# A transformer block on one core: exponentials behind the outputs, maxima ahead of them, a fifth stack, and operands at multiples of 128 bytes

## The chip, the cores and the metric

The kernel runs on one core of a Trainium2 chip. The metric is the device time of one launch in microseconds (us); lower is better. Before the change the median of three runs is 813.3 us (809.93 to 813.58).

## The reference: what is computed

One pre-norm transformer block in float32 on an input of 4 x 512 rows of 512. There are 32 heads of 16, with ALiBi slopes and a causal mask, and a gated feed-forward part with 1,376 inner columns. Cut to what matters:

```python
def block(x):
    n = layernorm(x)
    q, k, v = split(n @ w_attn + b_attn)                # 32 heads of 16
    s = einsum('bqhd,bkhd->bhqk', q, k) / 16
    s = where(rel <= 0, s + slopes * rel, -inf)         # rel = key - query
    x = x + einsum('bhqk,bkhd->bqhd', softmax(s), v) @ w_proj + b_proj
    n = layernorm(x)
    return x + (silu(n @ w_gate.T) * (n @ w_up.T)) @ w_down.T
```

## The kernel before

**Precision.** Every large product is made of three matmuls: each operand is split into a high and a low part (tiles of type float32r), and high x high, high x low and low x high are added in one PSUM bank. All matmuls are recorded under one helper, L86 (after the change L87), transposes under L89, so groups are told apart by tiles: xnT (normalized x, transposed), wqk_t, wrow_t (weights of v or of the projection), wf (feed-forward weights), c (q or k with bias), st (stacks), P (exponentials), v (values), aT (scaled heads), hl (the feed-forward part's inner rows).

**Units and steps.** A unit u (16 of them) is one batch and a quarter of the heads; each unit gives two steps su (32 in all, four heads each). A stack st holds, for the four heads of a step, rows of q and k and the rows that make the slopes and a coarse mask, so that one matmul of 64 rows gives the scores of a block. Two such matmuls, on rows 0 to 63 and 64 to 127, run side by side and write two banks. There are four stacks, used in turn.

**Two passes over the scores.** pass_a (L563) makes the scores of a step in five blocks of two banks each; VectorE adds the triangular mask and keeps each query's maximum (L582, into the tile M). Blocks 1 and 3 have 512 columns a bank, blocks 2 and 4 have 384 + 128, block 5 has 256 + 256. to_row (L590) transposes M on TensorE, copies it on ScalarE (tile mt) and writes it by a DMA on GpSimd's queue (L596) as one row into the step's stack. pass_b (L598) makes the scores again, transposed and with the maxima taken off by that row: five fills, each of two banks, two exponentials on ScalarE (L619) and two selects on GpSimd (L622) that clear what lies above the diagonal. Then av (L628) multiplies P with the values: 32 matmuls of a quarter of the array's columns (the outputs, tile U). Behind the outputs av issues what waits in `behind` (transposes of the next batch's x), the row of maxima of step su + 2, and the copy of U (tile ue) to DRAM.

**Jobs.** The projections of q, k and v and the output projection are jobs of 12 matmuls of 512 columns. Two jobs run as a pair (pair_steps, L362): each matmul is cut into two of 64 rows that run side by side, and the two jobs change their halves of the array in the middle. There a copy of one column (tile sync, L382) on ScalarE makes the second half wait for the first. in_step (L764) spreads the 24 pairs of matmuls over a step. qk_job (L401) ends with c in a high and a low part and sends it to DRAM (qd), from where load_stack (L513, on SyncE's queue) brings it into a stack; own_rows (L501, on GpSimd's queue) writes the rows that don't come from q and k.

**Heads and projection.** head_sums, inverses, attn_heads and scaled_heads read back U and the sums, multiply on GpSimd (uc by rb, L687), and make aT on ScalarE (L690) and VectorE (L691). proj_job (L457) adds bias and x.

**The feed-forward part.** For each batch, 11 tiles of gate, up and down weights (wf). Silu, product and the split into hl are L893, L897, L899 and L900; weights are loaded and split on the way (raw, L242 and L243). The first three tiles of the first batch run as pairs within steps 29 to 31, the others one matmul after another.

**What sets the order.** A list of events is written by hand: at(t, ...) gives each piece of work a time in units, of which a step has ten, and the events are issued in the order of these times. TensorE's instructions and SyncE's DMAs stay in that order (keep_in_program_order); on ScalarE, VectorE and GpSimd a scheduler may move what is not pinned. Each engine works through its queue in order. There are eight PSUM banks for everything. SBUF tiles come from pools; those that the change touches are t4 (c, xnT, aT, hl; 11 buffers of 4 KB a partition), P (13 of 2 KB), the stacks (4 of 8 KB), and the small tiles st (statistics, 24 bytes) and sync (4 bytes).

Within a step that starts at t0 = 10 su, the order in units is, before the change: block 1 of step su + 2 at -2.1, fill 1 at -0.9, block 2 at -0.2, the outputs of the step before at 0.5, then fill 2 (1.1), block 3 (2.1), fill 3 (3.1), block 4 (4.1), fill 4 (5.0), block 5 (6.0), fill 5 (6.9).

## Time and profile before

| what | value |
|---|---|
| runs (three) | 809.93, 813.58, 813.3 us; median 813.3 |
| the profiled execution | 814.1 us, of which the span from first to last instruction is 812.4 |
| mean granted clock of TensorE | 0.974 |
| attention: first outputs to last | 67.6 to 434.9 us of the span |
| feed-forward alone on TensorE | about 435 to 812 us |

Engines are PE = TensorE (PEld its weight loads), DVE = VectorE, ACT = ScalarE, POOL = GpSimd, SP = SyncE. Durations come from the one profiled execution. A busy time is a union: matmuls overlap, so one that is shown with 0.4 us may start 0.23 us after the one before. What a matmul costs is therefore read from the distance between starts. In views of stretches each engine's busy time stands before its number of records; then come the granted clock of TensorE (1.00 or 0.50 in single windows), the DMA share and GB/s. An idle time is shown with what ended it.

### The profile page before, as it was taken

The numbers are of one execution on the slowest core, as the hardware profiler recorded it, in microseconds if no ns is written. First come the engines' busy times: TensorE is split into PE (matmuls) and PEld (weight loads), VectorE is DVE, ScalarE is ACT, GpSimd is POOL, SyncE is SP. The second block draws the span as 40 slices with busy tenths as digits, with TensorE's granted clock in tenths as the row PEclk, the third lists the DMA queues.
The fourth block names the chain that finished last, engine by engine and source line by source line (L and its number), as shares of the span: only waits on it lengthen the run. The fifth ranks groups of instructions, "written<-read, shape, count | busy, mean of one in ns | idle before, by whom it ended". The sixth has DMA issues, their size and how long they took to land.

```text
span 812.4 us, 14957 instructions
## 1 busy us (share of the span) xinstructions
PE 779.6 (96%) x5272; PEld 587.4 (72%) x5272; DVE 458.5 (56%) x1441; ACT 343.0 (42%) x669; POOL 256.3 (32%) x560
## 2 busy tenths in 40 slices
PE   6998998999999999998999899999999999999997
PEld 5764755777777767765766688788887888788885
DVE  7798776988888888789833533621144121531212
ACT  4435665687656766674595322311112111211110
POOL 5415454666665566675533110000000000000000
PEclk9986998999999999998999999999999999999999
DMA  6444356458662776576335424221001101010001
GB/s 220 138 136 151 124 166 218 158 183 269 203 220 73 234 252 211 172 247 200 132 102 175 129 81 135 74 78 27 13 27 48 57 13 27 27 52 27 27 0 53
DMA packets 54764, 99.10 MB, mean 122 GB/s; under 512 B 13928, under 2 KB 14184, under 8 KB 54336
## 3 DMA queue, kind: packets, MB, share of 16 engines
q1 hardware_dynamic: 50464, 94.73, 35.9%
q0 software_dynamic: 4224, 3.40, 1.7%
q8 instruction: 42, 0.69, 0.3%
q14 instruction: 34, 0.28, 0.1%
HBM read 65.05 MB, written 32.77 MB: 120 GB/s over the span
## 4 chain that ended last, share of the span: by engine, by line
PE 84%; DVE 6%; DMA 3%; issue 2%; ACT 2%; POOL 2%; DVEq 0%; POOLq 0%; ACTq 0%
PE bank L86 81%; DVE bank L582 3%; PE bank L89 2%; DMA st<-mt 2%; ACT P L619 1%; DVE st L128 1%; DVE xt L145 1%; DVE M L582 1%; DMA ud<-ue 1%; POOL uc L687 0%; POOL P L622 0%; POOL r L135 0%; POOL xr L475 0%; DMA xt<-in_x 0%; DVE mv L129 0%
## 5 line engine op out<-in xcount | busy, mean ns | idle before, releaser
L86 PE MATMUL bank<-xnT,wf 128*128 128x512 f32 (+2 forms) x1128 | 270.7, 401 | 4.2 <-ACT sync L382 2.0
L582 DVE CUSTOM_DVE_ANT_0 bank<-bank,mask_t 128x512 f32<-128x512 f32 (+3 forms) x512 | 236.4, 520 | 35.0 <-PE bank L86 32.7
L86 PEld LDWEIGHTS bank<-xnT,wf 128*128 128x128 f32 (+2 forms) x1128 | 197.8, 188 | 54.1 <-ACT sync L382 2.7
L619 ACT ACTIVATE P<-bank 128x512 f32<-128x512 f32 x320 | 172.5, 598 | 66.9 <-PE bank L86 60.5
L86 PE MATMUL bank<-st 64*128 64x512 f32 (+3 forms) x1024 | 147.5, 327 | 13.9 <-DMA st<-mt 7.0
L897 DVE TENSOR_TENSOR sg<-sg,bank 128x512 f32<-128x512 f32 (+1 forms) x44 | 30.3, 688 | 208.8 <-PE bank L86 201.0
L622 POOL TENSOR_SCALAR_AFFINE_SELECT P<-P 128x256 f32<-128x256 f32 (+1 forms) x320 | 115.2, 366 | 102.5 <-ACT P L619 92.6
L86 PEld LDWEIGHTS bank<-st 64*128 64x128 f32 x1024 | 110.7, 190 | 44.9 <-DVE M L582 12.4
L86 PE MATMUL bank<-wf,hl 128*128 128x512 f32 (+1 forms) x528 | 136.2, 395 | 0.0
L86 PE MATMUL bank<-xnT,wqk_t 64*128 64x512 f32 (+1 forms) x720 | 116.9, 404 | 0.5 <-ACT sync L382 0.3
L86 PEld LDWEIGHTS bank<-wf,hl 128*128 128x128 f32 (+1 forms) x528 | 98.9, 188 | 23.5 <-issue 0.4
L893 ACT ACTIVATE sg<-bank 128x512 f32<-128x512 f32 (+1 forms) x44 | 26.3, 597 | 160.3 <-PE bank L86 160.2
L86 PE MATMUL bank<-P,v 128*32 128x512 f32 (+3 forms) x1024 | 84.8, 477 | 2.1 <-DVE M L582 1.8
L86 PEld LDWEIGHTS bank<-xnT,wqk_t 64*128 64x128 f32 (+1 forms) x720 | 72.0, 185 | 14.4 <-ACT sync L382 3.6
L899 ACT CAST hl<-sg 128x512 fp32r<-128x512 f32 (+1 forms) x44 | 27.3, 620 | 118.1 <-DVE sg L897 118.1
L582 DVE DVE_READ_ACCUMULATOR2_ANT M<- 128x1 f32 x512 | 72.1, 141 | 0.0
L133 POOL TENSOR_SCALAR ve<-mv 128x4 f32<-128x4 f32 x7 | 1.6, 225 | 209.1 <-DVE mv L129 209.1
L86 PEld LDWEIGHTS bank<-P,v 128*32 128x32 f32 x1024 | 32.2, 117 | 44.0 <-issue 36.8
L86 PE MATMUL bank<-wrow_t,aT 64*128 64x512 f32 (+1 forms) x336 | 63.8, 402 | 0.1
L86 PE MATMUL bank<-wrow_t,xnT 64*128 64x512 f32 (+1 forms) x336 | 59.1, 408 | 0.1
L900 DVE TENSOR_TENSOR hl<-sg,hl 128x512 fp32r<-128x512 f32 (+1 forms) x44 | 31.2, 710 | 28.2 <-ACT hl L899 27.8
L86 PEld LDWEIGHTS bank<-wrow_t,xnT 64*128 64x128 f32 (+1 forms) x336 | 37.9, 189 | 6.9 <-ACT sync L382 0.9
(77 smaller groups left out, 538.6 us busy)
## 6 DMA issues: line engine op xcount, KB each, us to landing
st<-qd SPq DMA_DIRECT2D x90, 256.0 KB, 3.8
qd<-c SPq DMA_DIRECT2D x30, 512.0 KB, 4.8
ud<-ue SPq DMA_DIRECT2D x32, 256.0 KB, 3.3
raw<-in_wgu SPq DMA_DIRECT2D x20, 256.0 KB, 3.2
xt<-in_x SPq DMA_DIRECT2D x16, 256.0 KB, 4.1
uc<-ud SPq DMA_DIRECT2D x16, 256.0 KB, 5.5
rb<-rd SPq DMA_DIRECT2D x16, 256.0 KB, 5.3
xr<-in_x SPq DMA_DIRECT2D x16, 256.0 KB, 4.7
```

The costliest lines, as they stand in the source:

```text
L86: tc.keep_in_program_order(nc.tensor.matmul(*args, **kw))
L89: tc.keep_in_program_order(nc.tensor.transpose(*args))
L128: pin(dve.bn_stats(st, xs[t]))
L133: pin(pool.tensor_scalar(ve, box["mv"][:, :, 1], EPS, None, ALU.add))
L145: dve.tensor_scalar(xs[t], xs[t], mv[:, t, 0:1], box["r1"][:, t : t + 1], ALU.subtract, ALU.mult)
L582: dve.tensor_tensor_reduce(s, s, mask_t[:, S - w : S], -1.0, 3.0e38, ALU.add, ALU.min, m[:, n : n + 1])
L619: act.activation(pt, p, AF.Exp)
L622: pool.affine_select(d, d, pattern=[[0, len(parts)], [1, 128]], compare_op=ALU.is_ge, fill=0.0, base=0, channel_multiplier=-1)
L893: act.activation(sg[:m], p, AF.Silu)
L897: dve.tensor_tensor(sg[:m], sg[:m], p, ALU.mult)
L899: act.copy(hl[:m, 0, :], sg[:m])
L900: dve.tensor_tensor(hl[:m, 1, :], sg[:m], f(hl[:m, 0, :]), ALU.subtract)
```

## The change

It has four parts.

1. The order in a step. Blocks of pass_a for step su + 2 move to -4.7, -2.5, -0.3, 0.9 and 3.1 units (relative to t0), the fills to 1.5, 2.6, 3.9, 4.9 and 6.3. So three blocks of two banks stand ahead of the outputs, and all five fills of a step behind the outputs of the step before.
2. Five stacks instead of four (NST), loaded for step su + 5 instead of su + 4, rows at t0 + 6.5 instead of 7.1 and q and k at t0 + 8.0 instead of 8.8. To make room, P has 12 buffers and t4 has 10.
3. One pair of jobs a step, in other steps than before. The pair of unit 3 is spread over step 0; the q and k of the next batch's four units lie in steps 2 to 5 of a batch (before: 2, 3, 4 or 5, and 9), the first two projections in steps 14 and 17, and 22 and 25 (before 13 and 14, 21 and 22), with the heads for them scaled 12 units later. Steps without a pair are 1, 6, 9 and 26; before, they were 1, 4, 6 and 26. From 280 units on the copy sync is made on VectorE. Some constants of the feed-forward part change: its first time (324.0 to 325.5), one weight load (318 to 314), and the times of the first three tiles' down matmuls (321, 323.9, 326.8 to 321, 331.3, 333.0).
4. The tiles st and sync are taken as 16 columns of which 6 and 1 are used, and an unused tile of 32 bytes, fill, is added. In the built program before, the tiles that matmuls read, ident and v apart, start 32 or 96 bytes past a multiple of 128 in their partition; after the change they start on one.

The arithmetic and the number of matmuls stay the same.

```diff
@@
-    'ffn': 324.0,
+    'ffn': 325.5,
...
-    't4': 11,
+    't4': 10,
...
-    'P': 13,
+    'P': 12,
@@ stats, norm
-            st = com.tile([128, 6], F32, tag="bst", bufs=2, name="st")
+            st = com.tile([128, 16], F32, tag="bst", bufs=2, name="st")[:, 0:6]
@@
+    cp.tile([128, 8], F32, name="fill")
@@ pair_steps
-                sync = com.tile([128, 1], F32, tag="sync", bufs=2, name="sync")
-                act.copy(sync, box["p"][1][:, 0:1])
+                sync = com.tile([128, 16], F32, tag="sync", bufs=2, name="sync")[:, 0:1]
+                (act.copy if clock["now"] < 280.0 else dve.tensor_copy)(sync, box["p"][1][:, 0:1])
@@
-    ST = [ph1.tile([128, 2, 2 * S], FR, name=f"st{n}") for n in range(4)]
+    ST = [ph1.tile([128, 2, 2 * S], FR, name=f"st{n}") for n in range(NST)]
@@ pass_b
-        for t, parts in zip((-0.9, 1.1, 3.1, 5.0, 6.9), fills):
+        for t, parts in zip((1.5, 2.6, 3.9, 4.9, 6.3), fills):
@@
+    at(1.0, load_stack, 4)
...
-    pairs(-1.8, 0.15, qk_job(3, 0), qk_job(3, 1))
@@
-        pass_a(su, (...)[su] if su < 2 else tuple(t0 - t for t in (22.1, 20.2, 17.9, 15.9, 14.0)))
+        pass_a(su, (...)[su] if su < 2 else tuple(t0 - t for t in (24.7, 22.5, 20.3, 19.1, 16.9)))
...
-        if su + 4 < NS:
-            at(t0 + 7.1, own_rows, su + 4)
-            at(t0 + 8.8, load_stack, su + 4)
+        if su + NST < NS:
+            at(t0 + 6.5, own_rows, su + NST)
+            at(t0 + 8.0, load_stack, su + NST)
@@
+        if not b:
+            in_step(0, qk_job(3, 0), qk_job(3, 1))
         if b:
             in_step(t, v_job(b, 2), v_job(b, 3))
-            in_step(t + 1, qk_job(4 * b + 3, 0), qk_job(4 * b + 3, 1))
         if b + 1 < B:
             xT_next(b + 1, 10.0 * (t + 1))
-            for n, s in enumerate((2, 3, 4 if b else 5)):
-                in_step(t + s, qk_job(4 * b + 4 + n, 0), qk_job(4 * b + 4 + n, 1))
+            for n in range(4):
+                in_step(t + 2 + n, qk_job(4 * b + 4 + n, 0), qk_job(4 * b + 4 + n, 1))
@@
-    for b, first, gap, s in ((0, 102.0, 5.0, 13), (1, 182.0, 5.0, 21), (2, 240.0, 5.5, 27)):
+    for b, first, gap, steps in ((0, 114.0, 5.0, (14, 17)), (1, 194.0, 5.0, (22, 25)), (2, 240.0, 5.5, (27, 28))):
...
-            in_step(s + n, proj_job(b, 2 * n), proj_job(b, 2 * n + 1))
+            in_step(steps[n], proj_job(b, 2 * n), proj_job(b, 2 * n + 1))
@@
-    for n, t in enumerate((262.0, 302.0, 271.0, 290.0, 318.0, 308.0)):
+    for n, t in enumerate((262.0, 302.0, 271.0, 290.0, 314.0, 308.0)):
@@ ffn
-            down(it, max(times[it] + PRM["ffs"] * 5 / 3, 321.0 + 2.9 * it))
+            down(it, times[it] + PRM["ffs"] * 5 / 3 if b or it >= PRM["fp"] else (321.0, 331.3, 333.0)[it])
```

More of the change, by code (lines that the diff above doesn't have):

```diff
@@ L27 @@
 KM = 47
+NST = 5
 FAR = -30000.0
@@ L176, in norm @@
             c = slice(t, t + 1)
-            st = com.tile([128, 6], F32, tag="bst", bufs=2, name="st")
+            st = com.tile([128, 16], F32, tag="bst", bufs=2, name="st")[:, 0:6]
             ov.bn_stats(st, xs[t])
@@ L501, in own_rows @@
     def own_rows(su):
-        st = ST[su % 4]
+        st = ST[su % NST]
         r0 = 8 * (su % 8)
-        assert su < 4 or used.get(su - 4) == 5
+        assert su < NST or used.get(su - NST) == 5
         for a in range(2):
@@ L507, in own_rows @@
             pin(pool.dma_start(to[3:16:4], cst[r0 + 4 * a : r0 + 4 * a + 4].rearrange("r (n c) -> r n c", n=2)))
-            if su < 4:
+            if su < NST:
                 pin(pool.dma_start(to[19:64:4], cst[64:76].rearrange("r (n c) -> r n c", n=2)))
-        if su >= 4:
+        if su >= NST:
             pin(pool.dma_start(st[KM : KM + 65 : 64, 0], cst[72:74, 0 : 2 * S]))
@@ L515, in load_stack @@
         u, s = divmod(su, 2)
-        assert {("qd", u, 0), ("qd", u, 1)} <= made and (su < 4 or used.get(su - 4) == 5)
+        assert {("qd", u, 0), ("qd", u, 1)} <= made and (su < NST or used.get(su - NST) == 5)
         src = qds[u].rearrange("n (e s l) c -> s e n (l c)", e=32, s=2)
-        st = ST[su % 4]
-        dma = (lambda *args: pin(sp.dma_start(*args))) if su < 4 else sp.dma_start
+        st = ST[su % NST]
+        dma = (lambda *args: pin(sp.dma_start(*args))) if su < NST else sp.dma_start
         for n, from_ in enumerate((slice(0, 4, 2), slice(0, 4, 3), slice(1, 3))):
@@ L556, in turn_stack @@
             own_rows(1)
-            for n in (2, 3):
+            for n in range(2, NST):
                 own_rows(n)
@@ L756, in block_kernel @@
         t0 = 10.0 * su
-        pass_a(su, ((-33.5, -19.5), (-19.0, -4.0))[su] if su < 2 else tuple(t0 - t for t in (22.1, 20.2, 17.9, 15.9, 14.0)))
+        pass_a(su, ((-33.5, -19.5), (-19.0, -4.0))[su] if su < 2 else tuple(t0 - t for t in (24.7, 22.5, 20.3, 19.1, 16.9)))
         if su < 2:
```

## The prediction

> **What bounds the kernel now.** I read the page first, then the spans step by step, then the waits of TensorE, then single stretches of its timeline.

> ```profile
> PE 779.6 (96%) x5272; PEld 587.4 (72%) x5272; DVE 458.5 (56%) x1441; ACT 343.0 (42%) x669; POOL 256.3 (32%) x560
> ...
> PEclk9986998999999999998999999999999999999999
> ```

> TensorE is busy for 96% of the span, so at most 33 us are idle. But busy time also holds matmuls at half clock, and matmuls that come more slowly than they could; the second row shows where the clock is cut. The next view cuts the span at the first output matmul (P,v) of each step. Columns: TensorE, weight load, VectorE, ScalarE, GpSimd busy, then clock.

> ```profile
> 102.60:110.90 8.30, 7.08 (x71) 4.10 (x67) 8.05 (x33) 6.70 (x15) 5.87 (x16) 1.00 0.70 249
> ...
> 123.50:133.70 10.20, 7.56 (x71) 4.44 (x70) 8.78 (x36) 6.90 (x15) 7.16 (x17) 0.91 0.88 293
> 133.70:148.40 14.70, 13.89 (x119) 9.04 (x120) 9.46 (x38) 7.62 (x17) 5.82 (x14) 0.83 0.34 122
> ...
> 195.80:208.00 12.20, 11.84 (x114) 8.82 (x115) 10.11 (x37) 8.60 (x18) 8.37 (x16) 1.00 0.55 182
> 208.00:219.00 11.00, 10.98 (x113) 8.64 (x113) 9.33 (x37) 6.79 (x15) 6.25 (x15) 1.00 0.66 213
> ...
> 419.50:432.60 13.10, 11.07 (x100) 7.67 (x101) 4.15 (x7) 10.76 (x19) 4.81 (x11) 0.87 0.54 156
> ```

> A step with a pair of jobs and no trouble takes 11.0 us, all of it TensorE (row 208.00); with eight transposes of x it takes 11.9. A step without jobs is bound by VectorE at about 8 us (row 102.60). What lies above these two values can be won by order: 3.7 us in row 133.70, some 2 in 123.50, 1.2 in 195.80, 2 in 419.50. The waits say why:

> ```profile
> PE bank L86 <- DMA st<-mt: 7.0, 4, 2.5
> PE bank L86 <- DVE M L582: 6.7, 13, 1.5
> PE bank L86 <- ACT sync L382: 2.3, 2, 2.0
> PE bank L86 <- ACT wf L242: 2.0, 1, 2.0
> ```

> The first row is the row of maxima on its way into the stack before an exponential's matmul may start; the last two are single stalls of 2.0 us at the end of attention. Such stalls are followed by a half clock:

> ```profile
> 132.52 1.22 PE L86 MATMUL bank<-st 64*128 64x512 f32 x6 [2.52 <-DMA st<-mt]
> 133.67 4.49 PE L86 MATMUL bank<-P,v 128*32 128x512 f32 x32
> ...
> 195.81 2.36 PE L86 MATMUL bank<-P,v 128*32 128x512 f32 x32
> ```

> The same 32 output matmuls take 4.49 us after the wait and 2.36 undisturbed. From 432.6 us on there is the feed-forward part, which TensorE alone sets.

> **The change, part by part.** All terms are against the profiled execution, 814.1 us (span 812.4).

> *(a) The row of maxima.* Before, the first exponentials of a step are placed 0.9 units before its start, 8.6 units behind the transpose of the maxima (10 units are a step). After, they are placed at +1.5, so 11 units behind, and the built order has them behind the previous step's outputs. The chain from transpose to landing was up to 0.3 + 0.6 + 5.4 us long (row DMA on the chain of waits); 11 units of a step without jobs are 8.8 us. So the waits of 1.11 and 2.52 us at 109 and 130 us go. What is late next is VectorE: it is busy for 8.05 of 8.30 and 8.78 of 10.20 us there, so only 0.3 + 1.4 = 1.7 us come out. The other two waits (1.78 at 65 us, 1.53 at 365 us) stand where VectorE is busy throughout: nothing. Of the clock, half-clock windows total 3.4 + 6.9 + 3.4 us behind these steps, but a window of 3.4 us also follows the jobless step at 68 us, whose longest idle time was 0.20 us. I keep one such window per jobless step (there are four before and after) and save 3.5 us at half, 1.7. Term: -3.4; ends 0 and -(7.0 + 6.9) = -13.9.

> *(b) End of attention.* From 280 units on the one-column copy between a pair's halves goes from ScalarE to VectorE, which is busy for 4.15 of 13.1 us there, where ScalarE has 10.76. In the built order the conversion (L242) of the fifth tile of gate and up weights stands ahead of a cast of hl (L899) on ScalarE, no longer behind it; that cast waits for the end of an up matmul. Both stalls lose their cause: 2.02 + 2.02 us, and the half-clock windows behind them (428.9 and 452.8 us, 3.4 us each) cost 3.4. The whole is 7.4; I take -6, since this tile is now wanted by the 53rd matmul after the last outputs instead of the 60th, 7 x 0.23 = 1.6 us earlier. Ends 0 and -7.4.

> [...]

> *(c) ScalarE waits for GpSimd's product uc in the two steps a batch that scale heads* (12.2 against 11.0 us; four such steps, and one at 346 us with 1.1 us). After, one scaling comes between the second and third exponentials, as unlucky as before, the other behind the last, where nothing urgent waits. Of 6 us I take a third, -2; ends 0 and -6.

> *(d) Three pairs of maxima's banks before the outputs.* In a step the order is now outputs, M's transpose, block 4, two exponentials, block 5, two exponentials, block 1 of the next stack, exponential, block 2, block 3. By the eight banks: at block 1 two are held by the jobs, two by block 5, four by exponentials, so it waits until VectorE has done block 5; a block costs VectorE 7.62/5 = 1.52 us (the step at 334.9 us has only the five blocks, 7.62 us), and an exponential's two banks cost ScalarE 2 x 0.6. Laid along the 11 us this gives a wait of 0 to 0.35 us a step, hidden where TensorE's queue gives way anyway. I take 0.1 x 28 = +3; ends 0 and +21 (third rival). Twelve P buffers serve ten a step, since outputs free them (2.36 us) before the second exponential writes; ten t4 buffers hold 4 xnT, 4 aT and 2 c at most. If that cover fails, c waits for its DMA, 4.8 us to landing, and holds two banks; the upper end takes this in. The stack loads and own rows are issued with 17 units in hand instead of 9, and GpSimd, past which they move, has 6 of 11 us: nothing. Moving the pair of jobs of unit 3 into step 0 takes work from the start, bound by VectorE (55 of 67.6 us), and adds one block, 1.5 us, that is saved later: 0, at most 3 either way.

> *(e) Operands at multiples of 128 bytes.* In the built program before, every large tile starts 32 or 96 bytes past such a multiple; after, all start on one. The trace shows what matmuls of 512 columns cost:

> ```profile
> 19.97 8.42 PE L86 MATMUL bank<-xnT,wqk_t 128*128 128x512 f32 x36
> 28.23 3.83 PE L86 MATMUL bank<-c,sel 128*128 128x512 f32 x16
> ...
> 525.54 5.66 PE L86 MATMUL bank<-xnT,wf 128*128 128x512 f32 x24
> ...
> 558.84 5.76 PE L86 MATMUL bank<-xnT,wf 128*128 128x512 f32 x24
> ```

> Start to start: (28.23 - 19.97)/36 = 229.4 ns and 229 for the second, where both operands have the same remainder (96 and 96, 32 and 32); 229 to 233.3 in the last two (32 against 96). Over 456 to 812 us the mean is 356.4/1,536 = 232 ns. At half clock 512 columns come 427 ns apart (eight in 3.55 us at 452.7 us), which is 213.3 at full clock: so 18.7 ns, or 8%, are lost to something that depends on full speed, and it grows with the columns. Whether placement is its cause no row tells, since no full-speed streamed operand starts on a multiple. Ends: 213.3, times the 1,560 matmuls of the feed-forward part and the last projection, -29 us, and up to -8 more in attention (34 streams a step, 0.6 us, 27 steps, half of it kept by VectorE); the slowest rows (240 ns, projection before a gate) +12. After, all remainders are equal, so I take the nearest rows, 229: 3 x 1,560 = -5.

> [...]

> *(f)* New constants of the feed-forward part move only its order around (b): 0.

> Sum: -3.4 - 6 - 2 + 3 - 5 = -13.4; 814.1 - 13.4 = 800.7. The execution stood 0.8 above the median of the runs: **800 us**.

> **Rivals.** *Placement gives all of the 8%:* 814.1 - 8.4 - 29 - 8 = 769, at the median 768. For it: the loss is the same 1 in 16 in short and long matmuls (256 columns: 116 instead of 107 ns) and vanishes at half clock, as if each 128 bytes cost one more access. Against: nothing in the trace ties it to the address.

> *The waits only change their place:* VectorE is the next in all jobless steps, the half clock stays, the placement does nothing: 814.1 - 2 = 812 (810 to 816).

> *Slower:* TensorE works in order, so block 3, now ahead of the outputs, holds them until VectorE has finished block 1. It decides when VectorE is over 1.7 us behind at block 1, since TensorE issues blocks 1 to 3 within 3.5 us. VectorE is busy for over 10 us in about half of the 28 steps (row 195.80 and those with norms). One block, 1.52 us, in 14 steps: +21 us, 801 + 21 = 822.

> **How the numbers follow.** Forecast 0.45, its own range 793 to 810; placement 0.25; no change 0.16; slower 0.14. The range 764 to 817 leaves out the slower case and some of the lowest. About 0.5%, 4 us, is what a measurement can tell from no change; that puts 0.04 of the forecast's own chance with "same": faster 0.41 + 0.25 = 0.66, same 0.20, slower 0.14.

> **What would show it.** (a): no wait for the row DMA; jobless steps near 8 us. (b): no idle time of 2 us from 410 to 460 us and clock 1.00 there. (c): at least two of the four steps at 11.0 us. (d): waits of TensorE for L582's maxima stay below 10 us. (e): the spacing in the feed-forward part, 229 by the forecast, 213 to 218 by the first rival, 232 by the second. A spacing above 235, or steps of 12 us throughout, would make the prediction wrong.

## The result, and the profile after

The change makes the kernel slower: 835.05 us median (four runs, 832.84 to 836.43) against 811.62 of the kernel before on the same chip; the ratio is 1.0276 with a 95% interval of 1.025 to 1.0302. The profiled execution took 836.4 us, its span 834.7. In all comparisons below, times are medians, and ratios are against runs of the kernel before on the same chip.

From the page of the kernel after, TensorE's row and its clock:

```profile
PE 791.3 (95%) x5272; PEld 594.5 (71%) x5272; DVE 459.6 (55%) x1445; ACT 338.4 (41%) x665; POOL 257.3 (31%) x561
...
PEclk9978999989999999998999999999999999999999
```

VectorE has the same amount of work as before (459.6 against 458.5 us busy), TensorE is busy for 11.7 us more and idle for 10.6 more. Windows at half clock total 46.8 us instead of 42.1, which costs some 2.3 us (an estimate: half the difference). So the time has gone into waits, a little into the clock, and the rest of the busy time into matmuls that come further apart. The first outputs come at 73.3 us instead of 67.6 (+5.7); from there to the last step's outputs it takes 382.5 us instead of 365.0 (+17.5); from there to the end 378.9 instead of 379.8 (-0.9). Together 22.3, the difference of the spans.

TensorE's waits after the change (what it waited for: us in all, times, longest):

```profile
PE bank L87 <- DVE M L585: 21.2, 20, 4.3
...
PE bank L87 <- ACT sync L385: 1.9, 2, 1.7
```

The wait for the row of maxima is gone, 7.0 us before. In its place stands the wait for VectorE's maxima: 21.2 us instead of 6.7. Stretches of steps after the change, with the columns of the prediction (TensorE, weight load, VectorE, ScalarE and GpSimd busy, then clock, DMA share and GB/s):

```profile
130.10:137.70 7.60, 7.19 (x67) 4.11 (x65) 7.52 (x31) 6.08 (x13) 3.95 (x11) 1.00 0.81 272
150.40:165.70 15.30, 13.04 (x118) 10.18 (x119) 11.84 (x49) 7.00 (x16) 7.84 (x26) 0.89 0.49 147
190.40:201.70 11.30, 11.30 (x115) 8.03 (x113) 9.06 (x36) 7.27 (x16) 5.81 (x15) 1.00 0.77 247
201.70:216.10 14.40, 12.67 (x119) 10.05 (x117) 9.73 (x38) 7.77 (x16) 8.01 (x18) 0.88 0.74 242
305.50:318.30 12.80, 11.07 (x115) 8.45 (x113) 9.71 (x36) 7.80 (x16) 7.09 (x16) 1.00 0.78 250
444.70:455.80 11.10, 10.17 (x100) 7.07 (x98) 4.17 (x8) 10.29 (x18) 2.76 (x9) 1.00 0.48 144
```

A step without jobs is short, as hoped (first row, 7.6 us). But an untroubled step with jobs takes 11.3 us and not 11.0 (third row; TensorE is busy throughout, and yet the step is longer). There are only six of these. Steps in which VectorE or ScalarE have more to do take 12.0 to 15.6 us. The second row holds a norm for the next batch. There, TensorE and then VectorE around 156 us:

```profile
155.17 0.64 PE L87 MATMUL bank<-wrow_t,xnT 64*128 64x512 f32 x4
158.06 0.75 PE L87 MATMUL bank<-st 64*128 64x256 f32 x4 [2.26 <-DVE M L585]
```

```profile
154.65 2.06 DVE L146 TENSOR_SCALAR xt<-xt,mv,r 128x512 f32<-128x512 f32 x4
156.64 0.55 DVE L585 CUSTOM_DVE_ANT_0 bank<-bank,mask_t 128x384 f32<-128x384 f32 x1
157.11 0.14 DVE L585 DVE_READ_ACCUMULATOR2_ANT M<- 128x1 f32 x1
...
158.74 0.43 DVE L585 CUSTOM_DVE_ANT_0 bank<-bank,mask_t 128x256 f32<-128x256 f32 x1 [0.48 <-PE bank L87]
```

TensorE stands for 2.26 us before block 5, whose bank VectorE still holds behind 2.06 us of norm; then VectorE stands for 0.48 us, since block 5 comes late. Both engines work in order, and each waits for the other: VectorE's own waits for TensorE before maxima grew as well, from 32.7 to 55.9 us.

In the feed-forward part the matmuls come as before, from start to start (553.65 - 548.08)/24 = 232.1 ns:

```profile
548.08 5.74 PE L87 MATMUL bank<-xnT,wf 128*128 128x512 f32 x24
553.65 2.95 PE L87 MATMUL bank<-wf,hl 96*128 96x512 f32 x12
```

### The profile page after: what moved, and what is told of

Its sections match the earlier page's. It is cut to its first block, busy times and chain, and to the rows that moved or that the text cites. A ratio compares the mean times of both kernels' runs of the same rounds, so it can differ in the third digit from the quotient of the medians.

```text
span 834.7 us, 14977 instructions
## 1 busy us (share of the span) xinstructions
PE 791.3 (95%) x5272; PEld 594.5 (71%) x5272; DVE 459.6 (55%) x1445; ACT 338.4 (41%) x665; POOL 257.3 (31%) x561
## 4 chain that ended last, share of the span: by engine, by line
PE 77%; DVE 9%; DMA 4%; POOL 3%; issue 2%; ACT 2%; SPq 1%; POOLq 0%; DVEq 0%; ACTq 0%
PE bank L87 75%; DVE bank L585 4%; PE bank L90 2%; POOL xr L478 1%; SPq L79 1%; DVE M L585 1%; DMA xr<-in_x 1%; DVE xt L146 1%; POOL uc L690 1%; ACT P L622 1%; DMA qd<-c 1%; DVE st L129 1%; DMA raw<-in_wgu 1%; DMA st<-qd 1%; DMA lc<-ud 1%
## 5 line engine op out<-in xcount | busy, mean ns | idle before, releaser
L585 DVE CUSTOM_DVE_ANT_0 bank<-bank,mask_t 128x512 f32<-128x512 f32 (+3 forms) x512 | 235.3, 521 | 58.7 <-PE bank L87 55.9
L87 PE MATMUL bank<-xnT,wf 128*128 128x512 f32 (+2 forms) x1128 | 266.2, 397 | 0.3 <-DVE sync L385 0.3
L622 ACT ACTIVATE P<-bank 128x512 f32<-128x512 f32 x320 | 168.2, 606 | 70.0 <-PE bank L87 67.9
L87 PE MATMUL bank<-st 64*128 64x512 f32 (+3 forms) x1024 | 168.3, 336 | 25.4 <-DVE M L585 19.5
L87 PEld LDWEIGHTS bank<-st 64*128 64x128 f32 x1024 | 120.6, 192 | 64.8 <-DVE M L585 34.7
L87 PE MATMUL bank<-wf,hl 128*128 128x512 f32 (+1 forms) x528 | 133.9, 395 | 0.0
L87 PE MATMUL bank<-xnT,wqk_t 64*128 64x512 f32 (+1 forms) x720 | 123.0, 415 | 0.3 <-ACT sync L385 0.3
L87 PEld LDWEIGHTS bank<-xnT,wqk_t 64*128 64x128 f32 (+1 forms) x720 | 75.7, 192 | 10.6 <-ACT sync L385 0.7
L87 PE MATMUL bank<-P,v 128*32 128x512 f32 (+3 forms) x1024 | 80.4, 456 | 1.6 <-DVE M L585 1.6
L87 PE MATMUL bank<-wrow_t,aT 64*128 64x512 f32 (+1 forms) x336 | 67.5, 413 | 1.8 <-ACT sync L385 1.7
L87 PE MATMUL bank<-wrow_t,xnT 64*128 64x512 f32 (+1 forms) x336 | 63.4, 424 | 0.0
```

The source lines that it names most:

```text
L87: tc.keep_in_program_order(nc.tensor.matmul(*args, **kw))
L585: dve.tensor_tensor_reduce(s, s, mask_t[:, S - w : S], -1.0, 3.0e38, ALU.add, ALU.min, m[:, n : n + 1])
L622: act.activation(pt, p, AF.Exp)
```

## Experiments: which part costs the time

**The old order in the kernel after.**

```diff
-tuple(t0 - t for t in (24.7, 22.5, 20.3, 19.1, 16.9))
+tuple(t0 - t for t in (22.1, 20.2, 17.9, 15.9, 14.0))
-zip((1.5, 2.6, 3.9, 4.9, 6.3), fills)
+zip((-0.9, 1.1, 3.1, 5.0, 6.9), fills)
```

> The kernel after with the five blocks of maxima and the five fills back at their old times (block 1 at -2.1, outputs at 0.5, fills from -0.9); five stacks, job steps, heads, end of attention and alignment stay as after (own rows and q, k are issued 0.6 and 0.8 units later, as before the change). Theory 'order' (three pairs of banks ahead of the outputs make TensorE and VectorE wait for each other in every step): the attention steps fall back by the 17.5 us that they grew, and the time is 812 to 818. Rival 'jobs' (the new job steps and the heads scaled 12 units later cost the time): it stays at 830 to 836.

829.5 us, ratio 1.0212 (1.0186 to 1.0238): neither, though close to the rival. The order isn't all; without it, the rest of the change still costs 17.4 us.

**The new order in the kernel before**: the same two lines the other way round, and what goes with them: five stacks loaded earlier (one a batch later, since its c is made later here), P 12, t4 10.

> The kernel before with only the new times of blocks and fills, and the five stacks, twelve P and ten t4 buffers that go with them (the stack of the last unit of a batch is loaded 6 units later, since its c is made later here). Theory 'order': slower than before by 12 to 20 us, 824 to 832. Rival 'jobs': 808 to 815.

835.2 us, 1.0286 (1.0253 to 1.0318), more than the 12 to 20 us expected. The order alone costs 23.0 us, as much as the whole change. So order and rest each cost about as much as both together: 23 and 17 make 23.

**Five stacks and fewer buffers alone, unit 3's pair alone, the new job steps alone, the end of attention alone.** The last two edits:

```diff
-            in_step(t + 1, qk_job(4 * b + 3, 0), qk_job(4 * b + 3, 1))
-            for n, s in enumerate((2, 3, 4 if b else 5)):
+            for n in range(4):
...
-((0, 102.0, 5.0, 13), (1, 182.0, 5.0, 21), (2, 240.0, 5.5, 27))
+((0, 114.0, 5.0, (14, 17)), (1, 194.0, 5.0, (22, 25)), (2, 240.0, 5.5, (27, 28)))
```

```diff
-                act.copy(sync, box["p"][1][:, 0:1])
+                (act.copy if clock["now"] < 280.0 else dve.tensor_copy)(sync, box["p"][1][:, 0:1])
...
```

The last one also has the change's constants: ffn 325.5, the weight load at 314, the times of the down matmuls.

> The kernel before with only the five stacks, 12 P and 10 t4 buffers, each stack loaded one step earlier (those of a batch's last unit 0.2 steps earlier only). The forecast's value, 0: 810 to 814. Rival 'buffers' (fewer P and t4 buffers, or own rows on GpSimd's queue at the wrong place): 818 to 830.

> The kernel before with only the pair of jobs of unit 3 spread over 7 to 90 tenths of step 0 (before: from -18 to 1.5 units). Theory: the start is bound by VectorE and ScalarE in order, and the late pair delays the conversions of c and the fills; first outputs at 71 to 73 us instead of 67.6, the time 815 to 818. The forecast's value: 812, at most 3 either way.

> The kernel before with only the new steps of the jobs from step 2 on, the projections in steps 14 and 17, 22 and 25, and their heads scaled 12 units later; old order, four stacks, unit 3 as before. With the old order, all other parts of the change together cost 17.4 us: 4.9 ahead of the first outputs, 13.5 in the steps, 3 less behind them. Theory 'heads' (the scaling of heads in steps 12 and 13, 20 and 21 now meets jobs whose conversions and sync wait behind it on ScalarE and VectorE): 820 to 826. Rival 'buffers' (five stacks, 12 P, 10 t4): 810 to 814.

> The kernel before with only the changes at the end of attention (sync on VectorE from 280 units on, the feed-forward part's first time, one weight load, the down matmuls of the first three tiles). The forecast's term (b): -6 us, so 805 to 807, no idle time of 2 us from 410 to 460 us. Rival (the waits only change place, as the idle 1.69 us at 376 us and the half clock at 538 us after the change suggest): 810 to 813.

Five stacks: 811.2, 1.0013 (0.9996 to 1.003), nothing that can be told from 0. Unit 3's pair: 816.5, 1.0074 (1.0049 to 1.0098), +6.0; first outputs at 72.3 us. Jobs: 826.3, 1.0196 (1.0171 to 1.0221), +15.9. End of attention: 812.3, 1.0006 (0.999 to 1.0023), nothing. The first of the two stalls of 2.02 us is there still, now 2.76 us; the second is gone, but TensorE stands for 1.58 us at 511 us instead, with a half-clock window behind it. A row of TensorE and then two of VectorE in that run:

```profile
426.85 1.43 PE L86 MATMUL bank<-xnT,wf 64*128 64x512 f32 x10 [2.76 <-DVE sync L382]
```

```profile
426.04 0.69 DVE L243 TENSOR_TENSOR wf<-raw,wf 128x512 fp32r<-128x512 f32 x1 [2.00 <-ACT wf L242]
426.65 0.15 DVE L382 COPY sync<-bank 128x1 f32<-128x1 f32 x1
```

The copy sync has left ScalarE's queue only to stand in VectorE's behind a subtraction (L243), which waits 2.00 us for ScalarE's conversion of the same weights.

**Alignment undone in the kernel after**: st and sync at 6 and 1 columns, no tile fill.

> The kernel after with st and sync at 6 and 1 columns and without the tile fill, so that operands again start 32 or 96 bytes past a multiple of 128. If alignment is worth what the forecast gave it, 5 us: 840. If it is worth nothing, as the spacing of 232 ns on both sides says: 834 to 836, spacing 232.

834.4 us, 1.0266 (1.0226 to 1.0306), against 1.0276 with it. The mean spacing of the two kinds of feed-forward matmuls (xnT by wf, wf by hl; full clock, pauses left out) is 232.2 and 232.5 ns, with it 232.3 and 232.1. Alignment is worth nothing here.

## Experiments: why the order is dear

**Two pairs of banks ahead instead of three.**

```diff
-tuple(t0 - t for t in (24.7, 22.5, 20.3, 19.1, 16.9))
+tuple(t0 - t for t in (24.7, 22.5, 19.2, 17.5, 16.0))
```

> The kernel after with block 3 behind the outputs again (0.8 units) and blocks 4 and 5 at 2.5 and 4.0, so that two pairs of banks stand ahead of the outputs instead of three. Theory of the forecast's slower rival (block 3 holds the outputs until VectorE is done with block 1): 822 to 828, the job steps without other work at 11.0 us again. Theory 'coupling' (every block that follows a fill at once waits for a bank that VectorE frees late, wherever the outputs stand): 830 to 836, and job steps at 11.3 us.

836.9 us, 1.032 (1.0299 to 1.0342); untroubled job steps take 11.5 us, not 11.0. Block 3's place isn't the cause, so the mechanism of the forecast's slower rival falls.

**Less work for VectorE, in both orders.** VectorE takes mask and maxima over the last 128 columns of each part alone ("light maxima"); TensorE's work stays the same.

```diff
+                    s = p[:, c0 + w - 128 : c0 + w]
-                    dve.tensor_tensor_reduce(s, s, mask_t[:, S - w : S], ...)
+                    dve.tensor_tensor_reduce(s, s, mask_t[:, S - 128 : S], ...)
```

> The kernel before, where VectorE takes mask and maxima over the last 128 columns of each part only (the maxima over all other columns are left out); TensorE's work is the same. Some 3.5 us of VectorE's 7.6 us a step are gone. Reference for the next run. Theory 'coupling' and its rival alike: start and jobless steps shorter, job steps still 11.0 us; 785 to 805.

> The kernel before with the new order and five stacks (835.2 us), with the same maxima left out. Theory 'coupling' (in the new order TensorE's blocks wait for banks that VectorE, working in order, frees late): most of the 23 us between the orders goes with VectorE's work, so this is at most 8 us above the run before it, and job steps are at 11.0 us. Rival (the order costs TensorE by itself, or by ScalarE's exponentials, which all stand in one group): 15 to 23 us above it.

803.8 (0.9913, 0.9885 to 0.994) and 807.8 us (0.9954, 0.9931 to 0.9978). With a lighter VectorE the orders are 4.0 us apart instead of 23. But the theory is met only in part: the first outputs come 5.4 us earlier in the new order (64.6 against 70.0 us), and the steps from there on still take 364.1 against 354.1 us. An untroubled job step is still 11.3 us long:

```profile
187.10:198.40 11.30, 11.26 (x114) 8.19 (x113) 5.58 (x28) 8.67 (x18) 6.68 (x14) 1.00 0.49 169
```

VectorE is busy for 5.58 us of it, so this isn't VectorE. What releases the second half of the jobs there is sync, on ScalarE, as a row of the weight loads in this step shows:

```profile
194.72 0.30 PEld L87 LDWEIGHTS bank<-xnT,wqk_t 64*128 64x128 f32 x4 [0.35 <-ACT sync L383]
```

In the kernel after, sync stands in the same place. ScalarE's rows of the kernel after, then those of TensorE and its weight load:

```profile
196.79 1.08 ACT L622 ACTIVATE P<-bank 128x512 f32<-128x512 f32 x2 [0.25 <-PE bank L87]
197.76 0.16 ACT L385 COPY sync<-bank 128x1 f32<-128x1 f32 x1
```

```profile
197.04 1.19 PE L87 MATMUL bank<-st 64*128 64x384 f32 x6
197.98 0.50 PE L87 MATMUL bank<-xnT,wqk_t 64*128 64x512 f32 x1
```

```profile
197.73 0.18 PEld L87 LDWEIGHTS bank<-st 64*128 64x128 f32 x1 [0.20 <-DVE M L585]
```

The first half of the jobs has been issued by 196.8 us, but sync stands behind the two exponentials of the third fill, and ends at 197.9. The six matmuls of fill 4 and block 1, which go at once before, take 0.94 us up to the next start. The last of them has itself waited for VectorE until 197.7 us, only 0.2 us before the end of sync. In the old order the third fill is 0.8 units earlier, with block 4 behind it.

**Earlier second and third fills, with full and with light maxima.**

```diff
-zip((1.5, 2.6, 3.9, 4.9, 6.3), fills)
+zip((1.5, 2.4, 3.4, 4.9, 6.3), fills)
```

> The kernel before with the new order (835.2 us), second and third exponentials at 2.4 and 3.4 instead of 2.6 and 3.9, so that sync, at 4.2, no longer stands right behind the third pair of exponentials on ScalarE. Theory 'sync' (the 0.33 us by which every job step is longer in the new order, with full and with light maxima, is the second half of the jobs waiting for sync behind two exponentials): job steps without other work at 11.0 us, 27 x 0.33 = 9 us gone, 825 to 828. Rival 'VectorE' (block 5 or 1 waits for banks just as long): 833 to 837.

> The kernel before with the new order, with both the maxima left out as in new_order_light_maxima (807.8 us) and the exponentials earlier as in new_order_fills_early (828.9 us). Theory 'two waits of equal length': with VectorE's and sync's wait both gone the job steps without other work are at 11.0 us and the time is 798 to 802. Rival (the group of fill 4 and block 1 without a job's matmul between costs TensorE itself 0.3 us): steps stay at 11.3, 805 to 808.

With full maxima 828.9 us, 1.0221 (1.0191 to 1.025): 6.3 less than the new order, but the untroubled steps stay at 11.3 to 11.4. The gain lies in two steps that scale heads (16.3 and 13.9 us become 12.2) and in one near the start of the last batch (14.8 become 11.3). So for the untroubled steps this run by itself speaks against sync. With light maxima too, 800.8 us, 0.99 (0.9863 to 0.9938), as the theory of two waits had it:

```profile
183.90:195.00 11.10, 11.10 (x118) 8.26 (x120) 6.39 (x36) 8.62 (x18) 7.76 (x16) 1.00 0.67 222
195.00:206.00 11.00, 10.97 (x114) 7.81 (x113) 7.42 (x44) 7.11 (x15) 6.25 (x16) 1.00 0.77 247
```

The steps are at 11.1 us, and all of them together take 353.5 us, where the old order with light maxima takes 354.1. So the new order costs TensorE nothing itself. It puts TensorE behind two other engines at once, by nearly the same time: one wait taken away shows nothing in an untroubled step, since the other is as long.

Over all steps it is otherwise. From the first outputs to those of the last step, in us:

| | old order | new order | new order, earlier fills |
|---|---|---|---|
| full maxima | 365.0 | 386.4 | 377.5 |
| light maxima | 354.1 | 364.1 | 353.5 |

The new order adds 21.4 us with full maxima, 12.5 with earlier fills, 10.0 with light maxima, and takes off 0.6 with both. Earlier fills so take back 8.9 and light maxima 11.4, and the two nearly add up. Most of the 21.4 lies in steps with more work than the untroubled ones: in before_new_order one with a norm takes 14.9 us instead of 11.5, one that scales heads 16.3 instead of 12.2.

**All first fills behind the outputs, blocks as before** (first time 0.8 instead of -0.9).

> The kernel before with the first exponentials of every step behind the outputs (0.8 instead of -0.9), blocks as before. Theory (the blocks ahead, and sync behind the third exponentials, make the order dear, not the first exponentials): 806 to 812. Rival (all exponentials in one group behind the outputs is what costs): 820 to 835.

814.8 us, 1.0047 (1.0025 to 1.0069): between the two. The start and the jobless steps get shorter (outputs of step 7 at 141.1 instead of 148.4 us); the sixteen job steps after that take 193.0 instead of 186.5, 0.4 us more each.

## Experiments: the jobs, the sum, and a faster kernel

**Heads two units earlier in before_jobs_only** (first 112.0 and 192.0 instead of 114.0 and 194.0).

> The run before_jobs_only (826.3 us) with the heads of the first two batches read and scaled 2 units earlier: at units 0 and 5 of steps 12 and 13, 20 and 21, as before the change in steps 11 and 12, 19 and 20; there a step with two scalings took 12.2 us, with units 2 and 7 it took 12.0 to 13.6, 12.9 and 12.3. Theory 'place in the step': 3 to 5 us of the 16 come back, 821 to 823. Rival 'which step' (what meets the scaling there, whatever its place): 825 to 828.

819.6 us, 1.01 (1.007 to 1.0129): 6.7 less. The three steps around the scaling of the first batch's heads take 12.2, 12.2 and 11.1 us instead of 12.0, 13.6 and 12.9. It is the place within the step.

**No bias sum on GpSimd for two tiles**, in that kernel; the sum is left out.

```diff
+            if b != 1 or t < 2:
                 pin(pool.tensor_tensor(box["xr"], box["xr"], bp_t, ALU.add))
```

> The run before_jobs_heads_early (819.6 us), with the bias sum of GpSimd (2.5 us in all) left out for the last two tiles of the second batch's projection, which the change moved from step 22 into step 25. Theory 'port' (that sum pushes GpSimd's products and selects into one unbroken row, in which a VectorE instruction with two operands in SBUF waits 3.1 us): that instruction is back at 0.75 us, the three steps from 359 us on lose 4 to 8 of their 46.0 us, 812 to 816. Rival (VectorE's norm alone makes these steps long): 818 to 821.

815.7 us, 1.0056 (1.0038 to 1.0073): 3.9 less, and the three steps from 359 us on take 40.4 instead of 46.0 us. With the sum, in before_jobs_heads_early, one of VectorE's instructions takes 3.90 us there, and TensorE waits for 2.86 us behind it. The same place in before_jobs_only (VectorE, GpSimd, TensorE):

```profile
369.20 3.91 DVE L691 SCALAR_TENSOR_TENSOR aT<-uc,bv_t,aT 128x512 fp32r<-128x512 f32 x1
```

```profile
368.62 1.27 POOL L622 TENSOR_SCALAR_AFFINE_SELECT P<-P 128x128 f32<-128x128 f32 x4
369.86 1.26 POOL L687 TENSOR_TENSOR uc<-uc,rb 128x512 f32<-128x512 f32 x1
371.08 1.48 POOL L622 TENSOR_SCALAR_AFFINE_SELECT P<-P 128x256 f32<-128x256 f32 x4
```

```profile
373.43 0.86 PE L86 MATMUL bank<-st 64*128 64x512 f32 x2 [3.17 <-DVE M L582]
```

Without the sum, the same instruction falls into a pause of GpSimd and takes 0.75 us, and no such wait follows:

```profile
362.00 0.75 DVE L692 SCALAR_TENSOR_TENSOR aT<-uc,bv_t,aT 128x512 fp32r<-128x512 f32 x1
```

Of the jobs' 15.9 us, 6.7 and 3.9 are so accounted for. Some 2 more lie in the step without jobs that moved from 4 to 9, where it holds eight transposes (steps 4, 5, 9 and 10 take 46.7 us together in before_jobs_heads_early, 44.7 before). The rest is open.

**Three causes undone in the kernel after**: unit 3's pair back, heads two units earlier, fills at 2.4 and 3.4.

> The kernel after (835 us) with three causes undone: unit 3's pair at its old time (-5.9 by itself before the change), heads of the first two batches 2 units earlier (-6.7), second and third exponentials at 2.4 and 3.4 (-9, if the run before it shows so). If they add up: 835 - 21 = 814, bounds 811 to 818. If they overlap, as the order (+23) and the rest (+17) did, which made 23 together: 822 to 830.

822.5 us, 1.0149 (1.0116 to 1.0181). That is some 12 us less than the kernel after, where the three gave 6.0, 6.7 and 6.3 one by one. They overlap, and the waits for VectorE stay (2.26 us in front of block 5 again).

**The first fill behind the outputs in a few steps only**, in the kernel before.

```diff
-zip((-0.9, 1.1, 3.1, 5.0, 6.9), fills)
+zip((0.8 if su in (2, 5, 7, 27) else -0.9, 1.1, 3.1, 5.0, 6.9), fills)
```

and, for the last kernel, `su < 8 or su in (26, 27)`.

> The kernel before with the first exponentials of steps 2, 5, 7 and 27 alone (those that follow the jobless steps and waited for the row of maxima) put behind the outputs, at 0.8 instead of -0.9. The forecast's term (a) by itself: -3.4 us, 808 to 810 beside 812, and the jobless steps near 8 us. Rival (VectorE or the next fill is the bound at once): 811 to 813.

> The kernel before with the first exponentials behind the outputs (0.8) in steps 0 to 7, 26 and 27 only, where fills_behind_only was shorter than before (141.1 instead of 148.4 us up to the outputs of step 7; 24.0 instead of 25.6 us in the two steps from 357 us on), and at -0.9 elsewhere, where it was 0.3 to 0.5 us a step longer. If these gains hold: 803 to 807. Rival (half-clock windows fall elsewhere and take them back): 808 to 811.

808.6 us, 0.9961 (0.9943 to 0.9979), and 807.8 us, 0.9959 (0.9945 to 0.9973). Among TensorE's waits in the first of them, the 7.0 us for the row of maxima have become:

```profile
PE bank L86 <- DMA st<-mt: 1.8, 1, 1.8
```

Both are faster than the kernel before, by 0.4%. The second isn't faster than the first by more than can be told: its profile has the same two half-clock windows of 3.41 us near 360 and 377 us, which that of fills_behind_only lacks.

## Why the prediction was wrong

The forecast was 800, with a range of 764 to 817; the time is 835. Two failures weigh most, and each alone puts the time above the range: the price of the three pairs of banks ahead in (d), and the new steps of the jobs, which got no price. Step by step:

- **(a), the row of maxima, -3.4: right.** The wait is gone, and the move of the first fill alone, on the old order, gives 811.0 - 808.6 = 2.4 by the medians, 0.39% or 3.2 us by the ratio. The jobless steps, foretold near 8, take 7.6 and 8.6, and 9.4 and 10.1 with eight transposes.
- **(b), the end of attention, -6: wrong as a term of its own.** By itself 0 (+0.06%). "Both stalls lose their cause" failed there for the first: VectorE's queue waits for ScalarE's conversion too. Together with the new order its sign came true: in the kernel after, TensorE has no idle time of 2 us from 410 to 460 us, and the clock is 1.00. The two steps before the last outputs take 20.9 us (23.4 before, 25.1 in before_new_order, which has the new order but the old end), and from there to the end it is 378.9 (379.8 and 379.3), though with a new idle time of 1.52 us at 535 us and a half-clock window behind it. So behind the new order the changes at the end may be worth up to 4.6 us; how much of that is (b) isn't shown, since the two kernels also differ in jobs and unit 3.
- **(c), scaling of heads, -2: wrong sign.** Those steps take 12.8 to 14.4 us. The forecast asked only which exponentials stand beside the scaling, and gave the new steps of the jobs no price, without a reason; alone they cost 15.9.
- **(d), three pairs of banks ahead, +3: mis-sized, and enough by itself.** Alone it costs 23.0, and the waits for maxima, which were to stay below 10 us, are 21.2 in the kernel after. The estimate of "0 to 0.35 us a step" was right in its upper end (0.32 in untroubled steps), but "hidden where TensorE's queue gives way anyway" was wrong: TensorE has nothing else to issue. Steps in which VectorE does norms or heads were left out of it; there TensorE stands 1.7 to 2.3 us. And sync was not followed on ScalarE's queue, though the third exponentials were moved up to it. That the upper end, +21, comes within 2 us of the 23.0 is luck: it was worked out from the rival's mechanism, block 3 ahead of the outputs, which fell.
- **Buffers, stacks, 0: right** (+0.13%, interval through 0). **Unit 3's pair, 0, at most 3: wrong**, +6.0; the start has no slack for it.
- **(e), alignment, -5: wrong**, 0. The rival with 8% falls too, and its argument had a wrong ratio: 18.7 of 213.3 ns is 1 in 11 and 9 of 107 is 1 in 12, not 1 in 16. What takes 18.7 ns of a matmul of 512 columns stays open.

The terms were added up, as if each had its own time. The runs show that they don't: order +23, jobs +16 and unit 3 +6 make 23 together. Why is shown in places only. The first outputs come 2.2 us later by the order, 4.6 by unit 3's pair, and 5.7 in the kernel after; the jobs' instruction of 3.91 us takes 0.75 us in the kernel after; and the changes at the end of attention seem to gain only behind the new order. The rest of the overlap is open. And the range left out the forecast's own upper bound of (d), to which it gave a chance of 0.14.

## What to carry to other kernels

When PSUM banks go round between engines that work in order, follow each bank and each small copy through the queue of the engine that frees it, in the heaviest step and not in the average one, before one calls a new order free. Two waits of equal length in one step hide each other: take both away before ruling either out. And price a moved job by the queue it lands in; here 2 of 10 units within a step were worth 6.7 us.

## What the hardware showed unexpectedly

```profile
210.49 0.57 PE L87 MATMUL bank<-st 64*128 64x512 f32 x2 [1.73 <-DVE M L585]
```

```profile
314.32 0.57 PE L87 MATMUL bank<-st 64*128 64x512 f32 x2 [1.73 <-DVE M L585]
```

The first lies within one window of the grid, and the next window is at half clock; the second is cut by the grid at 313.4 us into 0.81 and 0.92, and nothing follows (the rows 201.70 and 305.50 above: clock 0.88 and 1.00, 14.4 and 12.8 us). In these two profiles, from 20 us on, each of the 10 full-clock windows of the grid with 1.73 to 3.31 us idle on TensorE was followed by a half-clock one; of those not followed, none had more than 1.48. But 10 others were followed with less idle time, 0.05 to 1.69 us, so idle time isn't all that counts; what else does wasn't settled. So an edit that only shifts a stall may gain or lose such a window (an inference from the two steps above, where that is 1.6 us).

**A VectorE instruction beside GpSimd took 3.91 instead of 0.75 us.** In before_jobs_only it began at 369.20 us, within GpSimd's unbroken row of eight selects and a product (368.62 to 372.56), and ended at 373.1 us, 0.55 us after that row. It took 3.90 us in before_jobs_heads_early and 3.89 in after_old_order, beside the same row. In the kernel before, one of its 16 instructions of this line took 1.77 us; it began at 436.62 us, within a product on GpSimd (436.31 to 437.83), and ended 0.55 us after that. The other 15 there and all 16 in the kernel after took 0.74 to 0.76 us, although some ran beside selects on GpSimd for up to 0.26 us (at 388.27 us in the kernel after). None of these 31 began while GpSimd was in a select or a product; whether that decides it wasn't tested.
